# Slot sums of five tiles on VectorE in place of TensorE, 47 slots, and the weighting of three-slot units on ScalarE alone, in a graph attention kernel

One core of one Trainium2 chip. The metric is the device time of a whole execution, in microseconds, median of several runs; every run compared here is in the fast state (one run of e12 was over 1.5% above the fastest of its kernel and is left out of its ratio). A "point" is 1% of the time of before. "Before" and "after" are the kernels without and with the change.

## The reference

The reference is one layer of graph attention with a norm ahead of it, fp32 throughout, for 16 graphs (batches) of 1024 nodes with 512 features, 8 heads of 64. All batches share one adjacency matrix, which is sparse and has a few rows of high degree:

```python
_w = (1.0 + jnp.arange(1024)) ** -0.5; _w = _w / _w.mean()
_pij = jnp.clip(0.00390625 * _w[:, None] * _w[None, :], 0.0, 1.0)
adj = logical_or(uniform(1024, 1024) < _pij, eye(1024))
...
h = jnp.maximum(_layernorm(x), 0.0)
q, k, v = (h @ W + b for W, b in (Wq, Wk, Wv))            # as 8 heads of 64
scores = einsum('bihd,bjhd->bhij', q, k) / 8, where adj == 0: - 1e9
out = x + einsum('bhij,bjhd->bihd', softmax(scores), v)
```

## The kernel before

The kernel sorts the rows by degree, so that tile 0 (128 rows) holds the longest rows and tile 7 the shortest, and gives each tile as many neighbour slots as its longest row needs (`CAPS`). Lists of tile 0 that are longer still are cut into pieces of four, on 128 more rows (tile -1). One batch is 14 units of two to four slots. A unit passes these stations: GpSimd gathers one row of K and V per slot by an indirect DMA; VectorE multiplies K by the queries and sums over each head; ScalarE takes the exponent; VectorE (one slot) and ScalarE (the other slots) weight V; VectorE folds the slots into one; TensorE adds the units of a tile up in PSUM with an identity matrix; VectorE scales by the inverse row sum; GpSimd adds the input row and writes the output by an indirect DMA. Beside it TensorE projects the next batch.

```python
UNITS = ((7, 0, 2), (6, 0, 3), (5, 0, 4), (4, 0, 4), (3, 0, 3), (3, 3, 2), (2, 0, 3), (2, 3, 3),
         (1, 0, 4), (1, 4, 4), (0, 0, 4), (-1, 0, 4), (0, 4, 4), (0, 8, 4))     # tile, first slot, slots
BY_VECTOR = {2: 1, 3: 1, 4: 1}                # slots that VectorE weights
POOLS = dict(x=16, h=2, pht=1, hT=13, pkv=2, kvt=3, q=2, q0=1, g=5, acc=2, o=2)   # buffers

def fold(i, first, n):
    v = G[i][:, :, 1, :]
    nc.vector.tensor_tensor(v[:, 0:n], v[:, 0:n], v[:, first : first + n], ALU.add)
def add_up(i):                                # on TensorE
    ...
        nc.tensor.matmul(ACC[b, home], owner_t if t < 0 else ident, v[:, s, :], start=..., stop=...)
def row_sums(b, t):
    ...
    nc.vector.tensor_scalar(s, s, 2.0**-60, None, op0=ALU.max)
    nc.vector.reciprocal(INV[b, t], s)
def scale(b, t):
    nc.vector.tensor_mul(O[b, t]..., ACC.pop((b, t))..., INV.pop((b, t))...)   # per head
def residual(b, t):
    nc.gpsimd.tensor_tensor(O[b, t], O[b, t], X.pop(b * NT + NT - 1 - t), ALU.add)
def put_out(b, t):
    nc.gpsimd.indirect_dma_start(out=out_rows, out_offset=..., in_=O.pop((b, t))[:], ...)
```

The order in which every engine gets its instructions is not the order of the source. A planner (`Plan.ordered`) plays all steps through with guessed durations, priorities and buffer counts, and the kernel is emitted in the order that results. Each engine then works strictly in that order.

## Time and profile before

| | before |
|---|---|
| median of 3 runs | 1906.85 us (1903.21 to 1909.18) |
| TensorE, VectorE, ScalarE, GpSimd busy | 1764.5, 1749.3, 1420.9, 1292.4 us |
| mean granted TensorE clock | 0.983 |
| period of one batch in the middle | 110.2 us |

In lines of the profile PE is TensorE (PEld its weight loads), DVE is VectorE, ACT is ScalarE and POOL is GpSimd.

### The profile page before, as it was taken

The numbers are of one execution on the slowest core, as the hardware profiler recorded it, in microseconds if no ns is written. First come the engines' busy times: TensorE is split into PE (matmuls) and PEld (weight loads), VectorE is DVE, ScalarE is ACT, GpSimd is POOL, SyncE is SP. The second block draws the span as 40 slices with busy tenths as digits, with TensorE's granted clock in tenths as the row PEclk, the third lists the DMA queues.
The fourth block names the chain that finished last, engine by engine and source line by source line (L and its number), as shares of the span: only waits on it lengthen the run. The fifth ranks groups of instructions, "written<-read, shape, count | busy, mean of one in ns | idle before, by whom it ended". The sixth has DMA issues, their size and how long they took to land. (4 is left out here: it accounts for less than half of the span.)

```text
span 1906.6 us, 20253 instructions
## 1 busy us (share of the span) xinstructions
PE 1764.5 (93%) x4631; PEld 808.5 (42%) x4631; DVE 1749.3 (92%) x2330; ACT 1420.9 (75%) x5352; POOL 1292.4 (68%) x1244
## 2 busy tenths in 40 slices
PE   1799999999999999999999999999999999999884
PEld 0344444444444444444444444444444444444331
DVE  6759999999999999999999999999999999999995
ACT  2226777878788777877888787787778878777775
POOL 2616757677676867777676767778677767766673
PEclk9999999999999999999999999999999999999898
DMA  4628979888897988888898888889888888988873
GB/s 171 209 87 306 333 267 324 304 294 285 320 337 281 333 284 298 301 295 321 289 335 310 292 286 305 317 300 326 294 304 324 285 286 303 337 298 295 307 280 131
DMA packets 153951, 550.63 MB, mean 289 GB/s; under 512 B 18784, under 2 KB 18784, under 8 KB 153824
## 3 DMA queue, kind: packets, MB, share of 16 engines
q0 software_dynamic: 132224, 474.02, 71.0%
q1 hardware_dynamic: 21600, 75.24, 9.9%
q8 instruction: 39, 0.64, 0.1%
q14 instruction: 88, 0.72, 0.1%
HBM read 448.53 MB, written 100.66 MB: 288 GB/s over the span
## 5 line engine op out<-in xcount | busy, mean ns | idle before, releaser
L583 ACT ACTIVATE g<-g,weights 128x64 f32<-128x64 f32 x4352 | 1073.1, 338 | 0.0
L548 POOL DMA_INDIRECT g<-kv,index x768 | 763.2, 994 | 366.8 <-issue 247.7
L410 PE MATMUL pk<-wk,hT 128*128 128x512 f32 x1024 | 471.1, 604 | 0.0
L410 PE MATMUL pq<-wq,hT 128*128 128x512 f32 x1024 | 463.4, 596 | 0.0
L410 PE MATMUL pv<-wv,hT 128*128 128x512 f32 x1024 | 461.9, 594 | 0.0
L563 DVE TENSOR_REDUCE scores<-g 128x32 f32<-128x2048 f32 (+2 forms) x224 | 443.3, 1979 | 2.5
L558 DVE TENSOR_TENSOR g<-g,pq 128x2048 f32<-128x2048 f32 (+2 forms) x208 | 405.5, 1954 | 20.6 <-DMA g<-kv,index 14.6
L587 DVE TENSOR_TENSOR g<-g 128x512 f32<-128x512 f32 (+1 forms) x360 | 357.9, 994 | 7.9 <-ACT g L583 7.0
L602 PE MATMUL acc<-g,ident 128*128 128x512 f32 x538 | 274.8, 611 | 40.9 <-DVE g L587 33.0
L410 PEld LDWEIGHTS pk<-wk,hT 128*128 128x128 f32 x1024 | 200.0, 195 | 225.3 <-issue 221.2
L410 PEld LDWEIGHTS pv<-wv,hT 128*128 128x128 f32 x1024 | 195.8, 191 | 229.0 <-issue 225.6
L410 PEld LDWEIGHTS pq<-wq,hT 128*128 128x128 f32 x1024 | 196.5, 192 | 221.0 <-issue 217.4
L638 POOL DMA_INDIRECT out_dram<-o,perm x128 | 150.3, 1174 | 89.0 <-issue 68.8
L568 ACT ACTIVATE weights<-scores 128x32 f32<-128x32 f32 (+2 forms) x224 | 42.5, 190 | 223.9 <-DVE scores L564 223.5
L635 POOL TENSOR_TENSOR o<-o,x 128x512 f32<-128x512 f32 x128 | 165.1, 1291 | 23.0 <-DVE o L628 20.1
L366 POOL DMA_INDIRECT x<-in_x_dram,perm x128 | 143.8, 1124 | 53.0 <-issue 33.6
L602 PEld LDWEIGHTS acc<-g,ident 128*128 128x128 f32 x538 | 97.4, 194 | 146.2 <-issue 81.1
L577 DVE TENSOR_TENSOR g<-g,scores 128x512 f32<-128x512 f32 x224 | 152.3, 680 | 5.8 <-ACT scores L570 5.8
L393 ACT ACTIVATE h<-x,shift,rstd 128x512 f32<-128x512 f32 x128 | 103.5, 812 | 64.3 <-DVE shift L387 63.9
L421 ACT COPY kvt<-pk 128x512 f32<-128x512 f32 x128 | 73.4, 574 | 54.4 <-PE pk L410 48.3
L405 ACT COPY hT<-pht 128x512 f32<-128x512 f32 x128 | 74.4, 581 | 44.4 <-PE pht L400 44.4
L421 ACT COPY kvt<-pv 128x512 f32<-128x512 f32 x128 | 73.0, 570 | 45.7 <-PE pv L410 45.4
(149 smaller groups left out, 1036.8 us busy)
## 6 DMA issues: line engine op xcount, KB each, us to landing
kv<-kvt SPq DMA_DIRECT2D x128, 512.0 KB, 5.8
g<-kv,index POOLq DMA_INDIRECT x768, 6.3
adj<-in_adj_dram SPq DMA_DIRECT2D x8, 512.0 KB, 6.5
x<-in_x_dram,perm POOLq DMA_INDIRECT x128, 4.4
out_dram<-o,perm POOLq DMA_INDIRECT x128, 4.7
wk<-in_L_gnn_Wk_dram SPq DMA_DIRECT2D x1, 1024.0 KB, 11.2
wv<-in_L_gnn_Wv_dram SPq DMA_DIRECT2D x1, 1024.0 KB, 13.3
wq<-in_L_gnn_Wq_dram SPq DMA_DIRECT2D x1, 1024.0 KB, 12.7
```

What stands on the lines that cost most here:

```text
L366: nc.gpsimd.indirect_dma_start(out=X[n][:], out_offset=None, in_=x_rows, in_offset=on(ap=perm[:, t : t + 1], axis=0), element_offset=b * N * D
L410: nc.tensor.matmul(pt, HT[n][:, c, :], W[name][:, c, :], start=False, stop=(c == DC - 1))
L421: nc.scalar.copy(KVT[n][:, j, :], PT.pop((n, j)))
L548: nc.gpsimd.indirect_dma_start(out=G[i][:, s].rearrange("p j d -> p (j d)"), out_offset=None, in_=KV[b][:], in_offset=on(ap=index[:, c + s ...
L558: nc.vector.tensor_tensor(k, k, Q[b, t][:, None, :].to_broadcast([P, count, D]), ALU.mult)
L563: nc.vector.tensor_reduce(sc, heads(G[i][:, :count, 0, :]), AX.X, ALU.add)
L577: nc.vector.tensor_tensor(v, v, own.to_broadcast([P, n, H, HD]), ALU.mult)
L583: nc.scalar.activation(v[:, h, :], v[:, h, :], AF.Identity, scale=weights[:, c + s, h : h + 1])
L587: nc.vector.tensor_tensor(v[:, 0:n], v[:, 0:n], v[:, first : first + n], ALU.add)
L602: nc.tensor.matmul(ACC[b, home], owner_t if t < 0 else ident, v[:, s, :], start=(u == parts(home)[0] and s == 0), stop=(u == parts(home)[- ...
L635: nc.gpsimd.tensor_tensor(O[b, t], O[b, t], X.pop(b * NT + NT - 1 - t), ALU.add)
L638: nc.gpsimd.indirect_dma_start(out=out_rows, out_offset=on(ap=perm[:, t : t + 1], axis=0), in_=O.pop((b, t))[:], in_offset=None, element_o ...
```

## The change

The intent: TensorE and VectorE are level at the top; take the slot sums of tiles 7 to 3 off TensorE altogether (VectorE's fold leaves one slot per unit, so the scaling can read the gather buffer itself; the two units of tile 3 are joined by one more addition), and relieve VectorE by dropping the bound on row sums (one empty slot of weight 2^-60 per list does its work), one slot of 48, and the weighting of one slot in three-slot units, which goes to ScalarE. The planner is told, and replans; its guessed durations of folds and row sums change as well, which can move the order too (e4 below has these new guesses and is faster than before). The core of the diff:

```diff
-CAPS = (12, 8, 6, 5, 4, 4, 3, 2)
+CAPS = (11, 8, 6, 5, 4, 4, 3, 2)
-PIECES = 21
+PIECES = 17
-    (0, 8, 4),
+    (0, 8, 3),
+DIRECT = (7, 6, 5, 4, 3)
-BY_VECTOR = {2: 1, 3: 1, 4: 1}
+BY_VECTOR = {2: 1, 3: 0, 4: 1}
 ...  # in the plan
+        if by_vector(b, B, home):
+            acc = ("g", b * NU + parts[0])
+            added = weighed
+            if u != parts[0]:
+                added = [("join", i)]
+                add(("join", i), "DVE", 0.69, i + 1.5, weighed + summed, [g, acc])
+            summed = added
+        else:
+            add(("add_up", i), "PE", ...)
 ...
-    return {2: (), 3: ((2, 1), (1, 1)), 4: ((2, 2), (1, 1))}[count]
+    return {2: ((1, 1),), 3: ((2, 1), (1, 1)), 4: ((2, 2), (1, 1))}[count]
 ...
+def by_vector(b, B, t):
+    return t in DIRECT and b < B - 1
 ...
+        nc.gpsimd.memset(weights, 2.0**-60)
+        def join(i):
+            first = G[b * NU + parts_of(t)[0]][:, 0, 1, :]
+            nc.vector.tensor_tensor(first, first, G.pop(i)[:, 0, 1, :], ALU.add)
 ...
-            nc.vector.tensor_scalar(s, s, 2.0**-60, None, op0=ALU.max)
 ...  # in scale
+            if by_vector(b, B, t):
+                ACC[b, t] = G.pop(b * NU + parts_of(t)[0])[:, 0, 1, :]
```

More of the change, by code (lines that the diff above doesn't have):

```diff
@@ L39 @@
 SUM_MIN = 2.0**-30
-CAPS = (12, 8, 6, 5, 4, 4, 3, 2)
+CAPS = (11, 8, 6, 5, 4, 4, 3, 2)
 PIECE = 4
-PIECES = 21
+PIECES = 17
 LIST = CAPS[0] + PIECE * PIECES
+ROUNDS = -(-LIST // 8)
 UNITS = (
@@ L59 @@
     (0, 4, 4),
-    (0, 8, 4),
+    (0, 8, 3),
 )
+DIRECT = (7, 6, 5, 4, 3)
 UMAX = max(n for _, _, n in UNITS)
-SLOTS = sum(n for _, _, n in UNITS)
+SLOTS = sum(n for _, _, n in UNITS) + len(CAPS) + 1
 NU = len(UNITS)
 NT = len(CAPS)
-BY_VECTOR = {2: 1, 3: 1, 4: 1}
+BY_VECTOR = {2: 1, 3: 0, 4: 1}
 POOLS = dict(x=16, h=2, pht=1, hT=13, pkv=2, kvt=3, q=2, q0=1, g=5, acc=2, o=2)
@@ L171, in plan_of @@
         add(("list_of", t), "DVE", 2.6, -NU + 2 + 0.5 * t, [("sorted_rows", t)])
-    for k in range(LIST // 8):
+    for k in range(ROUNDS):
         add(("longest", k), "DVE", 2.4, -NU + 2.1 + 0.8 * k, [("longest", k - 1) if k else ("list_of", 0)])
-    add(("pieces",), "DVE", 9.0, -2, [("longest", LIST // 8 - 1)] + [("list_of", t) for t in range(NT)], [("pht", -1)], delay=1.0)
+    add(("pieces",), "DVE", 9.0, -2, [("longest", ROUNDS - 1)] + [("list_of", t) for t in range(NT)], [("pht", -1)], delay=1.0)
     for n in range(tiles):
@@ L217, in plan_of @@
         add(("exponent", i), "ACT", 0.4, i + 0.1, [("score", i)])
-        weighed = [("weigh_v", i)]
-        add(("weigh_v", i), "DVE", 0.15 + 0.533 * vector, i + 0.6, [("exponent", i)], [g])
+        weighed = []
+        if vector:
+            weighed.append(("weigh_v", i))
+            add(("weigh_v", i), "DVE", 0.15 + 0.533 * vector, i + 0.6, [("exponent", i)], [g])
         for s in range(count - vector):
@@ L223, in plan_of @@
         for n in folds(b, B, count):
-            add(("fold", i, *n), "DVE", 0.16 + 0.533 * n[1], i + 1.3, weighed, [g])
+            add(("fold", i, *n), "DVE", 0.2 + 0.6 * n[1], i + 1.3, weighed, [g])
             weighed = [("fold", i, *n)]
@@ L227, in plan_of @@
         acc = ("acc", b, home)
-        add(("add_up", i), "PE", 0.88 * (1 if folds(b, B, count) else count), i + 1.6, weighed, [g, acc])
-        parts = [v for v, (t_, _, _) in enumerate(UNITS) if max(t_, 0) == home]
+        parts = parts_of(home)
+        if by_vector(b, B, home):
[6 more added lines that the diff above has]
+        else:
+            add(("add_up", i), "PE", 0.88 * (1 if folds(b, B, count) else count), i + 1.6, weighed, [g, acc])
+            added = [("add_up", b * NU + v) for v in parts]
         if u == parts[-1]:
@@ L233, in plan_of @@
             sums = ("row_sums", b, home)
-            add(sums, "DVE", 0.6 if home else 1.2, i + 1, [("exponent", b * NU + v) for v in parts], [] if home else [("pht", -2, b)])
-            add(("scale", b, home), "DVE", 0.69, i + 1.8, [sums] + [("add_up", b * NU + v) for v in parts], [acc, o])
+            add(sums, "DVE", 0.4 if home else 1.0, i + 1, [("exponent", b * NU + v) for v in parts], [] if home else [("pht", -2, b)])
+            add(("scale", b, home), "DVE", 0.69, i + 1.8, [sums] + added, [acc, o])
             add(("residual", b, home), "POOL", 1.28, i + 2.5, [("scale", b, home)], [o, ("x", n)])
@@ L238, in plan_of, with parts_of @@
     return plan.ordered(POOLS)
+def parts_of(t):
+    return [u for u, (t_, _, _) in enumerate(UNITS) if max(t_, 0) == t]
+def by_vector(b, B, t):
+    return t in DIRECT and b < B - 1
 def folds(b, B, count):
@@ L437, in main_path @@
             col += count
+            if first + count == CAPS[tile_] or tile_ < 0:
+                col += 1
+        nc.gpsimd.memset(spot, 0.0)
         owner = const.tile([P, P], F32, tag="owner", name="owner")
@@ L448, in main_path @@
         ADJ = {}
-        found0 = const.tile([P, LIST + 1], F32, tag="found0", name="found_0")
+        found0 = const.tile([P, 8 * ROUNDS + 1], F32, tag="found0", name="found_0")
         def sorted_rows(t):
@@ L468, in longest @@
             nc.vector.max(found0[:, ts(k, 8)], row)
-            if k < LIST // 8 - 1:
+            if k < ROUNDS - 1:
                 nc.vector.match_replace(row, found0[:, ts(k, 8)], row, 0.0)
@@ L482, in pieces @@
             nc.tensor.matmul(before, below, count, start=True, stop=True)
-            begin = found[:, LIST : LIST + 1]
+            begin = found[:, 8 * ROUNDS : 8 * ROUNDS + 1]
             nc.vector.tensor_copy(begin, before)
@@ L491, in pieces @@
             nc.scalar.copy(owner_t, p_ot)
-            width = LIST + 1 - CAPS[0]
+            width = 8 * ROUNDS + 1 - CAPS[0]
             p_list = ps_h.tile([P, width], F32, tag="pht", name="p_list")
-            nc.tensor.matmul(p_list, owner, found[:, CAPS[0] : LIST + 1], start=True, stop=True)
+            nc.tensor.matmul(p_list, owner, found[:, CAPS[0] :], start=True, stop=True)
             part = once.tile([P, 1], F32, tag="part", name="part")
@@ L568, in exponent @@
             nc.scalar.activation(weights[:, w, :], scores[:, w, :], AF.Exp, scale=HD**-0.5)
-            own = scores[:, c + count - BY_VECTOR[count] : c + count, :]
-            nc.scalar.activation(own, own, AF.Exp, scale=HD**-0.5)
+            if BY_VECTOR[count]:
+                own = scores[:, c + count - BY_VECTOR[count] : c + count, :]
+                nc.scalar.activation(own, own, AF.Exp, scale=HD**-0.5)
         def weigh_v(i):
@@ L587, in fold @@
             nc.vector.tensor_tensor(v[:, 0:n], v[:, 0:n], v[:, first : first + n], ALU.add)
-        def parts(t):
-            return [u for u, (t_, _, _) in enumerate(UNITS) if max(t_, 0) == t]
+        def join(i):
+            b, t, w, c, count = unit(i)
+            first = G[b * NU + parts_of(t)[0]][:, 0, 1, :]
+            nc.vector.tensor_tensor(first, first, G.pop(i)[:, 0, 1, :], ALU.add)
         def add_up(i):
@@ L597, in add_up @@
             home = max(t, 0)
-            if u == parts(home)[0]:
+            if u == parts_of(home)[0]:
                 ACC[b, home] = ps_a.tile([P, D], F32, tag="acc", name=f"acc_{b}_{home}")
@@ L605, in add_up @@
                     v[:, s, :],
-                    start=(u == parts(home)[0] and s == 0),
-                    stop=(u == parts(home)[-1] and s == count - 1),
+                    start=(u == parts_of(home)[0] and s == 0),
+                    stop=(u == parts_of(home)[-1] and s == count - 1),
                 )
@@ L612, in row_sums @@
             c = first_col[t, 0]
-            nc.vector.tensor_reduce(s, weights[:, c : c + CAPS[t], :].rearrange("p s h -> p h s"), AX.X, ALU.add)
+            nc.vector.tensor_reduce(s, weights[:, c : c + CAPS[t] + 1, :].rearrange("p s h -> p h s"), AX.X, ALU.add)
             if t == 0:
@@ L645, in main_path @@
             sorted_rows, list_of, longest, pieces, load_x, stats, variance, power, shift, norm, flip, unflip, proj_kv, evict_kv,
-            store_kv, queries, copy_q, gather, multiply, score, exponent, weigh_v, weigh_s, fold, add_up, row_sums, scale,
+            store_kv, queries, copy_q, gather, multiply, score, exponent, weigh_v, weigh_s, fold, join, add_up, row_sums, scale,
             residual, put_out,
```

## The prediction

> **What bounds the kernel now.** First the page's table of busy time per engine.
>
> ```profile
> PE 1764.5 (93%) x4631; PEld 808.5 (42%) x4631; DVE 1749.3 (92%) x2330; ACT 1420.9 (75%) x5352; POOL 1292.4 (68%) x1244
> ```
>
> TensorE and VectorE are level, so a change that relieves only one of them should give little. The shares mix the start and the end with the middle, so I next asked for the busy time of each engine between 300 and 1700 us.
>
> ```profile
> core 0: us, PE busy (x) PEld busy (x) DVE busy (x) ACT busy (x) POOL busy (x), PEclk, DMA share, GB/s
> 300.00:1700.00 1400.00, 1359.79 (x3606) 625.52 (x3605) 1332.06 (x1750) 1115.27 (x4224) 1014.97 (x967) 0.99 0.86 306
> ```
>
> In the middle TensorE is busy 97.1%, VectorE 95.1%, ScalarE 79.7%, GpSimd 72.5% and the DMA engines 86%. To turn shares into time I need the period of one batch. One multiply per batch reads the queries of the split rows, so its starts, in the view of the gathered tile, mark the batches:
>
> ```profile
> L558 DVE TENSOR_TENSOR g<-g,pq_-1_1306 x1: 2275/2275/2275, 228.4 to 228.4; 128x2048 f32<-128x2048 f32 x1
> ...
> L558 DVE TENSOR_TENSOR g<-g,pq_-1_8974 x1: 2275/2275/2275, 1221.8 to 1221.8; 128x2048 f32<-128x2048 f32 x1
> ```
>
> Nine batches in 993.4 us: 110.4 us each. Of that TensorE is busy 107.2 and idle 3.2, VectorE busy 105.0 and idle 5.4, ScalarE busy 88.0. The waits of TensorE between 200 and 1780 us say what its small idle time is:
>
> ```profile
> PE acc L602 <- DVE g L587: 33.0, 11, 4.1
> PE p_more L619 <- DVE more L617: 6.0, 3, 2.1
> PE pq L408 <- DVE g L558: 3.8, 8, 0.6
> ```
>
> It waits for VectorE's folds, rarely. TensorE, in its fixed order, sets the pace, with VectorE 2 us per batch behind it.
>
> **What the skill says.** The Trainium skill, "TensorE: Matmul & The Clock Gate", section "Wait — 56ns, not 53.3ns?", gives a warm start-to-start of 215.7 ns for 512 columns. The trace shows an fp32 slot sum as two records, and this timeline shows what the pair occupies:
>
> ```profile
> 902.09 1.02 PE L602 MATMUL acc<-g,ident 128*128 128x512 f32 x2
> 902.95 0.60 PE L400 MATMUL pht<-ident,h 128*128 128x128 f32 x4
> ```
>
> The next matmul starts 0.86 us later, which is four times the skill's figure. I use 0.86, not the 2 x 611 ns of the group's mean durations, which overlap.
>
> "SBUF — State Buffer", section "Who interferes with whom", says that a VectorE instruction with two SBUF inputs contends with a GpSimd instruction that reads SBUF, and that `tensor_scalar` can enter a 2-port mode that contends too; the loser blocks. The trace agrees. The fold reads SBUF twice, the weighting reads SBUF and PSUM:
>
> ```profile
> L587 DVE TENSOR_TENSOR g<-g x360: 656/686/2873, 156.4 to 1801.0; 128x1024 f32<-128x1024 f32 x120, 128x512 f32<-128x512 f32 x60
> ...
> L577 DVE TENSOR_TENSOR g<-g,scores x224: 654/680/689, 147.3 to 1881.5; 128x512 f32<-128x512 f32 x112
> ```
>
> The weighting never takes over 0.689 us, the fold up to 2.873. The group means below hold these blocks, so I cost with means.
>
> "ScalarE: Activation LUTs", section "What ACT_TABLE_LOAD costs", says that an ACTIVATE costs a fixed part plus 0.833 ns per element and that back-to-back ones overlap by about 93 ns. In the trace one takes 338 ns, and a slot of eight takes 1.92 us (from 649.15 to the next instruction at 651.07), 240 ns each: 98 ns of overlap, in agreement.
>
> ```profile
> 649.15 2.01 ACT L583 ACTIVATE g<-g,weights 128x64 f32<-128x64 f32 x8
> 651.07 0.56 ACT L421 COPY kvt<-pk 128x512 f32<-128x512 f32 x1
> ```
>
> **The change part by part.** The durations, from the groups by shape:
>
> ```profile
> L587 DVE TENSOR_TENSOR g<-g 128x512 f32<-128x512 f32 x240 | 181.9, 758 | 1.3 <-ACT g L583 0.7
> L587 DVE TENSOR_TENSOR g<-g 128x1024 f32<-128x1024 f32 x120 | 176.0, 1467 | 6.6 <-ACT g L583 6.3
> ...
> L577 DVE TENSOR_TENSOR g<-g,scores 128x512 f32<-128x512 f32 x224 | 152.3, 680 | 5.8 <-ACT scores L570 5.8
> ...
> L628 DVE TENSOR_TENSOR o<-acc,inv 128x512 f32<-128x512 f32 x128 | 87.6, 684 | 6.2 <-PE acc L602 5.9
> ...
> L622 DVE TENSOR_SCALAR sums<-sums 128x8 f32<-128x8 f32 x128 | 50.4, 394 | 4.4
> ```
>
> The instruction orders of both kernels, compared by kind, give the counts.
>
> TensorE. In batches 0 to 14 the sums of tiles 7 to 3 went through it: 2 (two slots, unfolded) + 1 + 1 + 1 + 3 (one folded unit, one of two slots) = 8 fp32 matmuls per batch, 120 in all; one more goes in the last batch with the 48th slot. The orders agree: 269 become 148. 8 x 0.86 = 6.9 us per batch, 121 x 0.86 = 104 us in all. Nothing is added to TensorE.
>
> VectorE, per batch. Removed: eight bounds on row sums at 0.394 = 3.15. They are long because the 0.17 us instruction is blocked at times (median 0.172, longest 2.987). Five weightings of three-slot units (four units before, and the unit that shrinks from four slots to three) at 0.60, their spacing when they run back to back (0.68 less an overlap of 0.08) = 3.0. One slot of multiply and score: 2.284 less 1.749 and 2.281 less 1.756 = 1.06. A four-slot fold becomes a three-slot one: a wide and a narrow fold (1.467 + 0.758) become two narrow ones, 0.71. Added: folds of the two units of two slots, 2 x 0.758 = 1.52; the join of tile 3's two units, 0.758; five scalings that now read SBUF twice, by estimate as slow as a fold, 5 x (0.758 - 0.684) = 0.37. Net -7.92 + 2.65 = -5.3 us per batch. So VectorE takes over the sums and still loses work, since the bound and the weighting leave it at the same time. In the start two rounds of maximum and replacement go, 4 x 1.21 = 4.8 us.
>
> ScalarE. Four more slots per batch (34 become 38) x 1.92 = 7.7, less five small exponents that add 0.08 each to the spacing = 0.4: +7.3 us per batch, 117 in all. 88.0 becomes 95.3, still below the others.
>
> GpSimd and DMA. 16 fewer gathers of 768, at about 1.25 us per issue: 1.25 us per batch. The DMA share falls in bytes by 1.5% and rises per us as the period shrinks.
>
> Per batch TensorE then has 107.2 - 6.9 = 100.3, VectorE 105.0 - 5.3 = 99.7, ScalarE 95.3. If TensorE keeps its 3.2 of idle time, the period is 103.5; if VectorE keeps its 5.4, it is 105.1. I choose 104.6, nearer VectorE's, because it now owns more of the path and its waits for ScalarE get longer: a gain of 5.8 over 15 batches, 87 us. The shorter list at the start is worth some 2 of its 4.8, as TensorE is busy by then with projections of its own. The end costs some 4: the last batch still adds up on TensorE without folds, and from 1867 us on ScalarE runs there without a pause; its slots grow from 34 to 38, 7.7 us, of which I take half to be visible. 1906.9 - 87 - 2 + 4 = 1822; I say 1820.
>
> **The rivals.** (1) VectorE becomes the bound and gives the gain back: the scalings and joins read SBUF twice and are followed at once by GpSimd's residual (1.29 us), which reads SBUF as well. If each of the 8 new or changed instructions per batch is blocked for 0.3 us more, the period is 107.5 and the time about 1865. Against it: the folds, in the same neighbourhood, lose only 78 ns on average (758 against 680), and eight blocked bounds disappear. (2) ScalarE at 91% of the new period delays evictions and norms, so that TensorE waits for projection buffers: perhaps 2 us per batch, 1850. For it: 7.3 us more work in a fixed order, and units of three slots now wait for three slots in a row (5.8 us). Against it: TensorE has almost no waits for ScalarE now (1.5 us). (3) All waits fall: gathered buffers of direct tiles come free after VectorE's scaling rather than after TensorE's queue, on which the gathers waited 27.9 us in all, and TensorE's 33.0 us of waits for folds shrink with fewer sums. Then the full 104 us show, with the start: about 1798. (4) The gathers hide everything: at 86% DMA share already, 91% of a 104.6 us period. Against it: VectorE waits only 14.6 us in all for gathered data.
>
> **Range and chances.** TensorE's whole relief at the low end and rival 2 at the high end give 1795 to 1855. Faster by over 2% means below 1868.7, which even rival 1 would just pass; so 0.93. Within 2% needs two rivals at once, 0.06. Slower would need a fall into the slow general path or a broken pipeline; the row lists hold 79 neighbours and 128 pieces, and I counted at most 66 and 116 in the inputs, so 0.01.
>
> **What would show it.** Right: TensorE's busy time near 1660 us, VectorE's near 1660 (1749 less 15 x 5.3 and 4.8), ScalarE's near 1540; a period near 104.6 between the multiplies of the split rows; the scaling from SBUF near 0.76 us on average; the bounds gone. The step on VectorE is wrong if folds, joins and scalings average well above 0.76, the step on ScalarE if TensorE's waits for it exceed 20 us, the step on the end if the last batch takes over 10 us longer. The sum is wrong altogether if TensorE's idle time in the middle grows beyond 6 us per batch.

## More of the kernel before

From the view of VectorE's waits and from that of GpSimd's, kernel before, whole run (engine, tile and line; what ended the wait; us in total, times, longest):

```profile
DVE g L558 <- DMA g<-kv,index: 14.6, 4, 12.8
```

```profile
POOL out_dram L638 <- issue: 68.8, 49, 5.0
```

VectorE hardly ever waits for gathered rows. GpSimd stands 68.8 us ahead of output writes, and the profile sees nothing that it waits for ("issue"); the experiments show what it is in the kernel after.

## The result, and the profile after

| | before | after |
|---|---|---|
| median (runs of the same rounds, 4 each) | 1905.38 us | 1898.20 us |
| ratio, 95% interval | | 0.9956 (0.9934 to 0.9978) |
| mean granted clock | 0.983 | 0.969 |

The change is worth 0.4%, not 4.5%; the time lies outside the range. A ratio here and below is the mean time of one kernel's runs over that of before's runs of the same rounds, so it isn't quite the ratio of the medians; the ratios of the experiments also leave out the first, profiled run of each kernel.

The table of busy time of the kernel after, and its busy time between 300 and 1700 us (us, TensorE, weight loads, VectorE, ScalarE, GpSimd; clock; DMA share; GB/s):

```profile
PE 1682.0 (89%) x4343; PEld 766.7 (41%) x4389; DVE 1657.1 (88%) x2161; ACT 1529.8 (81%) x5784; POOL 1271.2 (67%) x1230
```

```profile
300.00:1700.00 1400.00, 1293.06 (x3353) 591.95 (x3390) 1264.95 (x1621) 1199.87 (x4565) 997.98 (x958) 0.97 0.83 302
```

The work left the engines as planned: VectorE fell by 92 us to 1657 (1660 was predicted), ScalarE rose to 1530 (1540), TensorE fell by 82 us to 1682 (1660; 46 of its 4389 matmul records are missing, so it is somewhat more). But they now stand idle instead: in the middle TensorE is busy 92.4% (97.1 before) and VectorE 90.4% (95.1). (37 of 3390 matmul records are missing in this window; at 0.43 us each, half of the 0.86 us pair, they would add about 1%, an estimate.) The batches' marks, the multiplies of the split rows, say so most directly:

```profile
L586 DVE TENSOR_TENSOR g<-g,pq_-1_1284 x1: 2281/2281/2281, 220.9 to 220.9; 128x2048 f32<-128x2048 f32 x1
...
L586 DVE TENSOR_TENSOR g<-g,pq_-1_8941 x1: 2273/2273/2273, 1212.6 to 1212.6; 128x2048 f32<-128x2048 f32 x1
```

Nine batches in 991.7 us: 110.2 us each, as before (110.4 over nine; over fourteen, 110.2 before and 110.0 after). **The period did not move.** The 14 us by which the span shrank are elsewhere: the first mark comes 7.5 us earlier, fourteen periods give 2.5, and the last batch and the end about 4.

What stands in the relief's place? First the waits of TensorE from 200 to 1780 us, then, over the whole run, the wait of VectorE for gathered rows and those of GpSimd ahead of output writes:

```profile
PE acc L634 <- DVE g L616: 43.3, 25, 6.2
PE acc L634 <- issue: 20.1, 7, 4.8
PE acc L634 <- ACT g L612: 12.1, 4, 4.5
PE pk L433 <- ACT hT L428: 9.9, 12, 1.7
PE pht L423 <- ACT h L416: 9.4, 7, 3.0
```

```profile
DVE g L586 <- DMA g<-kv,index: 99.9, 44, 13.9
```

```profile
POOL out_dram L670 <- issue: 98.6, 58, 5.5
...
POOL out_dram L670 <- DMA out_dram<-o,perm: 21.5, 7, 3.9
```

TensorE waits for everybody, VectorE waits seven times as long for gathered rows as before, and GpSimd waits longer ahead of output writes. Those go round in a ring: no row is gathered before a buffer is free, no buffer is free before VectorE has folded, and GpSimd issues the gathers behind its output writes. A view of waits can't say which link of such a ring is the guilty one. This piece of GpSimd's timeline (start, us, idle before it) shows one candidate:

```profile
597.84 2.51 POOL L667 TENSOR_TENSOR o<-o,x 128x512 f32<-128x512 f32 x2
600.51 1.29 POOL L670 DMA_INDIRECT out_dram<-o,perm  x1 [0.17 <-POOL o L667]
605.53 0.98 POOL L670 DMA_INDIRECT out_dram<-o,perm  x1 [3.73 <-issue]
```

Two output writes in a row: the second one stands still for 3.73 us after the first has been issued. In the built program every output write carries a wait for the DMA of the output write before it, since both write the same tensor. Counted from the order of GpSimd's instructions, the plan before has 2 such neighbours among its 127, the plan after 20; the idle time of GpSimd right ahead of output writes (gaps over 0.45 us, less 0.3 each) is 54 us before and 109 us after.

Last, the disputed costs on VectorE (count, total us, mean ns):

```profile
L616 DVE TENSOR_TENSOR g<-g 128x512 f32<-128x512 f32 x285 | 233.2, 818 | 5.2 <-ACT g L612 5.1
L616 DVE TENSOR_TENSOR g<-g 128x1024 f32<-128x1024 f32 x105 | 139.2, 1326 | 4.7 <-ACT g L612 4.5
...
L660 DVE TENSOR_TENSOR o<-g,inv 128x512 f32<-128x512 f32 x75 | 50.6, 674 | 5.3 <-DMA out_dram<-o,perm 5.0 <-issue 0.2
...
L622 DVE TENSOR_TENSOR g<-g,g 128x512 f32<-128x512 f32 x15 | 10.2, 683 | 0.0
```

The scaling from SBUF takes 674 ns, not the 758 of the prediction, and the join 683. The instructions that the change added are not slow.

### The profile page after: what moved, and what is told of

It is laid out like the page before. It is cut to its first block, busy times and chain, and to the rows that moved or that the text cites. A ratio compares the mean times of both kernels' runs of the same rounds, so it can differ in the third digit from the quotient of the medians.

```text
span 1892.6 us, 19830 instructions
## 1 busy us (share of the span) xinstructions
PE 1682.0 (89%) x4343; PEld 766.7 (41%) x4389; DVE 1657.1 (88%) x2161; ACT 1529.8 (81%) x5784; POOL 1271.2 (67%) x1230
## 5 line engine op out<-in xcount | busy, mean ns | idle before, releaser
L612 ACT ACTIVATE g<-g,weights 128x64 f32<-128x64 f32 x4864 | 1195.8, 338 | 1.5
L576 POOL DMA_INDIRECT g<-kv,index x752 | 751.9, 1000 | 341.3 <-issue 227.2
L586 DVE TENSOR_TENSOR g<-g,pq 128x2048 f32<-128x2048 f32 (+2 forms) x208 | 397.0, 1913 | 104.5 <-DMA g<-kv,index 99.9
L591 DVE TENSOR_REDUCE scores<-g 128x32 f32<-128x2048 f32 (+2 forms) x224 | 433.9, 1937 | 2.7 <-ACT scores L599 1.2
L616 DVE TENSOR_TENSOR g<-g 128x512 f32<-128x512 f32 (+1 forms) x390 | 372.4, 955 | 9.8 <-ACT g L612 9.6
L634 PE MATMUL acc<-g,ident 128*128 128x512 f32 x296 | 166.2, 658 | 95.3 <-DVE g L616 42.2
L634 PEld LDWEIGHTS acc<-g,ident 128*128 128x128 f32 x296 | 53.5, 201 | 172.6 <-issue 90.5
L423 PE MATMUL pht<-ident,h 128*128 128x128 f32 x512 | 82.9, 287 | 34.8 <-ACT h L416 34.0
L423 PEld LDWEIGHTS pht<-ident,h 128*128 128x128 f32 x512 | 66.5, 148 | 110.8 <-issue 53.7
L606 DVE TENSOR_TENSOR g<-g,scores 128x512 f32<-128x512 f32 x144 | 97.8, 680 | 4.0 <-ACT weights L596 2.4
```

The lines of the kernel that those rows point to most:

```text
L423: nc.tensor.transpose(PH[n][:, c, :], hn[:, ts(c, P)], ident)
L576: nc.gpsimd.indirect_dma_start(out=G[i][:, s].rearrange("p j d -> p (j d)"), out_offset=None, in_=KV[b][:], in_offset=on(ap=index[:, c + s ...
L586: nc.vector.tensor_tensor(k, k, Q[b, t][:, None, :].to_broadcast([P, count, D]), ALU.mult)
L591: nc.vector.tensor_reduce(sc, heads(G[i][:, :count, 0, :]), AX.X, ALU.add)
L612: nc.scalar.activation(v[:, h, :], v[:, h, :], AF.Identity, scale=weights[:, c + s, h : h + 1])
```

## The experiments

Theories: A, the output writes in pairs hold GpSimd. B, ScalarE is too full. C, VectorE's instructions with two SBUF inputs collide with GpSimd's. D, five gather buffers are too few. E, TensorE's idle time lowers its clock. F, the planner's order as a whole is at fault; G, the path of the data through VectorE is. H came later (see there).

The runs e1 to e10 and e13 to e16 were on one chip (13), e11 and e12 on a second (2), e17 and e18 on a third (10), none known to be that of the result. Each ratio is against runs of before on the same chip (medians 1922 to 1932 us).

**The kernel after, unchanged**, as the point that others are compared with.

> The changed kernel itself, unaltered, so that the experiments have it on their own chip. If chips agree: 0.996 of the kernel before. If theory A still holds and this chip is only worse for the changed kernel: 1.03 or more, as the run with side outputs was at 1.012 of before on the chip of the first four experiments.

1963.03 us, 1.0209 (1.0184 to 1.0233): on this chip the change makes the kernel 2% slower, where the first chip had it 0.4% faster. Before itself lost 0.9 to 1.0% between the two. The pattern is that of the first chip, with more idle time: TensorE busy 1272 of 1400 us (1293 there), clock 0.96 (0.97), 104 us of idle time ahead of output writes (109) and 177 ahead of gathers (119). So a gain or loss of two points of this kernel isn't a property of the code alone, and below only ratios of one chip are set against each other, but for the two kernels that were repeated.

**Output writes that don't wait for each other** (A). Tiles 1 to 7 write to DRAM tensors of their own; the order of instructions is kept, and the result is wrong.

```diff
-out=out_rows, ..., element_offset=b * N * D
+out=SIDE[t][:] if t else out_rows, ..., element_offset=0 if t else b * N * D
```

> The changed kernel, every instruction in the same order, but the outputs of tiles 1 to 7 go to seven separate buffers in device memory, so that a write of an output no longer waits for the write before it to land (wrong result on purpose). Theory A (GpSimd stands still for those landings, 110 us of gaps before output writes against 54 us before the change, and the gathers behind them come late): the gaps fall below 30 us, VectorE's wait for gathered data falls from 100 to below 40 us, the time to 1830 to 1860. Theory B (ScalarE, which got 7.3 us per batch more, delays TensorE): the gaps fall, the time stays above 1885. Theory C (VectorE's two-input reads collide with GpSimd): as B.

1943.38 us, 1.0124. The idle time ahead of output writes fell from 104 us to 2, so the waits are indeed those of one write for another, and VectorE's wait for gathered rows fell from 78 to 39.5 us. But 0.85 points, less than half of what A expected, is all that came of the 100 us: the idle time ahead of gathers rose from 177 to 265 us. What GpSimd waits for there isn't shown; free buffers are the likely reason.

**No two output writes in a row** (A, correct result). The planner makes each output write follow the one before it.

```diff
-[("residual", b, home)], [o], delay=4.0, moves=0.75)
+[("residual", b, home)] + ([put] if put else []), [o], delay=4.0, moves=0.75)
+put = ("put_out", b, home)
```

> The changed kernel with one more rule in the planner: an output write is placed only when the one before it has landed. Same instructions, other order, right result; no two output writes stand next to each other on GpSimd (20 pairs do in the changed kernel). Theory A: GpSimd's gaps before output writes fall from 110 us to below 50, time 1840 to 1870. Theories B and C: within 0.5% of the changed kernel, about 1895.

1945.97 us, 1.0108, no neighbours left, idle time ahead of output writes 23 us. It agrees with e1: theory A holds for about one point of the loss, and no more; the time that it had forecast wasn't reached.

**The weighting of three-slot units shared again** (B). `BY_VECTOR[3] = 1`, as in before.

> The changed kernel with one slot of each three-slot unit weighted on VectorE again (80 weightings back, 48 us; ScalarE loses 80 x 1.92 = 154 us). Theory A: no gain, 1895 to 1915, as the output writes are still in pairs (23). Theory B: faster, 1850 to 1875, because ScalarE is relieved. Theory C: 1895 to 1910.

1964.65 us, 1.0213 against 1.0209. ScalarE was relieved by 143 us (1534 to 1391 busy) and nothing came of it. By itself this doesn't settle B, since VectorE got 61 us more work (1718) and the plan changed too (23 neighbours among the output writes). The next run does: it leaves ScalarE at 1528 us and is far faster. Theory B falls, though TensorE's waits for ScalarE had grown.

**All sums on TensorE, the rest of the change kept.** `DIRECT = ()`; the planner replans.

> The changed kernel with the slot sums of all tiles on TensorE again (two-slot units still folded, no bound, 47 slots, three-slot units on ScalarE). TensorE gets 6 matmuls x 0.86 = 5.2 us per batch back, 77 us in all; output writes stand apart again (1 adjacent pair). Theory A: GpSimd's gaps before output writes back to about 55 us, time 1870 to 1890, not slower than the changed kernel although TensorE does more. Theory B: slower than the changed kernel or equal, 1895 to 1915, as ScalarE's load is the same. Theory C: faster than the changed kernel, 1860 to 1890, with the mean of a fold back from 818 to about 760 ns.

1883.98 us, 0.9792 (0.9771 to 0.9812): without its headline the change is worth 2.1%. Its window from 300 to 1700 us:

```profile
300.00:1700.00 1400.00, 1362.77 (x3630) 625.09 (x3629) 1267.20 (x1642) 1219.60 (x4658) 1005.73 (x969) 1.00 0.85 306
```

TensorE is busy 97.3% at full clock here. So five tiles' sums on VectorE cost 4.2 points on this chip, with all that they do to the plan.

**Six gather buffers** (D), two other pools made smaller for the room. The planner replans.

```diff
-hT=13, pkv=2, kvt=3, ... g=5
+hT=11, pkv=2, kvt=2, ... g=6
```

> The changed kernel with six buffers for gathered units in place of five (two fewer for transposed rows and one fewer for stored rows, which make the room). Theory D (the ring of gathered buffers sets the pace: on average 4.4 of 5 are held in the changed kernel, a unit holds one for 34 us): period falls toward 104 us per batch, time 1800 to 1850. Theory A alone: some gain, as this plan also has no two output writes next to each other, 1860 to 1880. If neither holds, about 1895.

1920.13 us, 0.9982, 2.3 points better than after. But the new plan also has no output writes in a row, so this run alone doesn't separate the buffer from the order.

**Direct sums for one-unit tiles only.** `DIRECT = (7, 6, 5, 4)`: no join.

> The changed kernel with direct sums for tiles 7, 6, 5 and 4 alone; tile 3, whose first buffer waits through the join for its second unit, goes back to TensorE (2 matmuls per batch, 26 us). Theory D: the long hold of that buffer (41.7 us against a mean of 34.2) is gone, time 1870 to 1890. Theory A: 15 adjacent pairs of output writes are left of 20, time within 0.5% of the changed kernel.

1949.97 us, 1.0154, 0.55 points better than after. The plan has 15 neighbours among its output writes in place of 20; the join is not the main cost.

**TensorE kept busy** (E). The kernel after in its own order, plus one constant fp32 matmul on TensorE, read by nobody, for each of the 90 sums that left it (batches 0 to 14, one per unit).

```diff
+nc.tensor.matmul(WARM[b, home], ident, W["q"][:, 0, :], start=..., stop=...)
```

> The changed kernel, all engines in the same order, plus 6 fp32 matmuls per batch (90 in all, 77 us) of constant data on TensorE where the slot sums used to stand; nobody reads their result. Theory E (TensorE's time is no longer on the path, and its idle gaps lower its granted clock, 0.97 against 0.99): time within 0.5% of the changed kernel or up to 1% faster, clock back at 0.98 or more. If TensorE were still the bound: slower by up to 77 us, 1960 to 1975.

1979.82 us, 1.030, 0.9 points slower than after. 90 x 0.86 = 77 us of work were added to TensorE and the time rose by 17, so TensorE's work isn't what the others follow here, for the most part. (The idle sums also take turns with the real ones in two buffers of PSUM, which may be a part of the 17.) E's own expectation was missed too: the time is more than 0.5% longer, and the clock rose from 0.961 to 0.969 only, not to 0.98.

**Order against path of the data** (F, G). Two runs cross them. e9: direct sums, but every instruction in the order that the planner makes for sums on TensorE; a join stands where the second unit's sum stood. e10: the order of the kernel after, but with sums on TensorE.

```diff
 # e9
+for key in plan.ordered(POOLS):           # planned as if all sums were on TensorE
+    if key[0] == "add_up" and by_vector(b, B, home):
+        if u == parts_of(home)[0]: continue
+        key = ("join", key[1])
+    order.append(key)
```

> The work of the changed kernel (direct sums for tiles 7 to 3) in the order that the planner made for the kernel with all sums on TensorE (0.979 of before); on each engine every other instruction stands where it stands there, and a join stands where the add-up stood. Theory F (the direct sums themselves cost nothing; the planner's order for them is worse, among other things because it knows nothing of output writes waiting for each other): 0.96 to 0.98 of before. Theory G (the data path is worse: VectorE holds the gathered buffers, reads SBUF twice, and must do itself what TensorE did beside it): 1.00 to 1.03 of before, as the changed kernel on this chip (1.021).

> The other corner: the order that the planner made for the changed kernel, but the sums of tiles 7 to 3 done on TensorE right after the last fold, and scaled from PSUM. Theory F: as slow as the changed kernel or slower, 1.02 to 1.04 of before (TensorE has 5.2 us per batch more). Theory G: near 0.98 of before, as with the other order.

| ratio on chip 13 | sums on VectorE | sums on TensorE |
|---|---|---|
| in the order of after | 1.0209 (e5) | 1.0552 (e10) |
| in the order of the plan for TensorE | 0.9863 (e9) | 0.9792 (e4) |

The windows of e9 and e10:

```profile
300.00:1700.00 1400.00, 1317.62 (x3448) 598.77 (x3447) 1242.10 (x1650) 1214.71 (x4636) 1019.68 (x964) 0.98 0.86 304
```

```profile
300.00:1700.00 1400.00, 1281.97 (x3290) 578.94 (x3290) 1183.05 (x1498) 1119.47 (x4237) 920.02 (x885) 0.96 0.78 279
```

**The order is worth 3.5 points with the same direct sums, and 7.6 with the same sums on TensorE.** That is theory F in the main, though e9 lies a little above its range (0.98) and e10 above its own. One reserve belongs to the 7.6: the order of after has no place for the sums on TensorE, and e10 puts each right behind its fold, so TensorE's waits for folds there (60.8 us between 200 and 1780 us, 6.5 in e4) can be the placement's. The 3.5 has no such flaw. In the better order the direct sums still give nothing against e4 (+0.7 points), though TensorE has 77 us less to do. TensorE stands at 91.6% in e10 with exactly the work that makes it 97.3% busy in e4.

**The better order with six buffers**, sums on TensorE (e11) and direct (e12).

> The rest of the change with the sums on TensorE (0.979 on this chip with five gather buffers), now with six gather buffers of 16 KB (one from the transposed rows, 13 to 11, and one from the projections' rows, 3 to 2). If the ring of gathered buffers (D) is what still holds this version: 0.965 to 0.972, with TensorE over 97% busy in the middle. If this version is at TensorE's limit already (it was 97.3% busy in the middle at a clock near 1.00): 0.975 to 0.985, no gain, and more gather buffers held without effect. If the planner's order for six buffers happens to be a bad one: above 0.99.

> The direct sums in the order that the planner makes for the sums on TensorE, with six gather buffers (the order of the run beside it). If direct sums have been held by the ring and by the order together, this is the version where TensorE's 77 us fewer should show at last: 0.955 to 0.97, and it beats the run beside it. If TensorE's work no longer sets the pace and the loop from gather to fold does even with six buffers: 0.98 to 0.99, as the direct sums with five buffers in the same kind of order (0.986), and equal to or slower than the run beside it.

1863.13 us, 0.9662 (0.9618 to 0.9706), and 1923.24 us, 0.9941 (0.9864 to 1.0017). The windows of e11 and of e12:

```profile
300.00:1700.00 1400.00, 1379.02 (x3652) 636.98 (x3704) 1301.68 (x1670) 1248.51 (x4765) 1040.21 (x993) 1.00 0.88 313
```

```profile
300.00:1700.00 1400.00, 1305.82 (x3374) 598.26 (x3411) 1287.10 (x1631) 1202.75 (x4583) 998.17 (x957) 0.97 0.86 303
```

e11 lies where D expected it, is correct and beats before by 3.4%, with TensorE 98.5% busy. Against e4 it gains 1.3 points, from chip to chip and in a new plan, so the buffer and the order aren't separated here any more than in e6. e12 lies outside both expectations: with six buffers the direct sums lose 2.8 points at one and the same order. That miss led to the next theory. The two runs were repeated on a third chip:

> The sums on TensorE with six buffers again, unchanged. On another chip it was 0.966. If the gain of the one-input residual there (0.954) was the edit's: 0.963 to 0.969 on the same chip, so the edit is worth about 1.2 points. If it was the chip's: 0.952 to 0.957.

> The direct sums in the other order with six buffers again, unchanged. On another chip it was 0.994. If the gain of the one-input residual (0.963) was the edit's: 0.985 to 0.998 on the same chip. If it was the chip's: 0.960 to 0.970.

1861.90 us, 0.9644, and 1919.75 us, 0.9964, both in the range for "the edit's" (the edit is that of e14 and e15 below). These two kernels keep their ratios within 0.3 points from chip to chip.

**What differs between e11 and e12 on VectorE** are the same instructions at different lengths. From the groups by shape, the folds of e11, and then e12:

```profile
L616 DVE TENSOR_TENSOR g<-g 128x512 f32<-128x512 f32 x285 | 204.2, 717 | 11.1 <-ACT g L612 4.9 <-issue 2.2 <-ACT weights L596 2.1
L616 DVE TENSOR_TENSOR g<-g 128x1024 f32<-128x1024 f32 x105 | 128.4, 1223 | 6.5 <-ACT g L612 6.0 <-issue 0.5
```

```profile
L626 DVE TENSOR_TENSOR g<-g 128x512 f32<-128x512 f32 x285 | 218.9, 768 | 11.6 <-remote 5.9 <-ACT g L622 4.9 <-issue 0.2
L626 DVE TENSOR_TENSOR g<-g 128x1024 f32<-128x1024 f32 x105 | 152.7, 1454 | 4.2 <-ACT weights L606 1.8 <-ACT g L622 1.7 <-issue 0.6
L670 DVE TENSOR_TENSOR o<-g,inv 128x512 f32<-128x512 f32 x75 | 61.7, 823 | 0.0
L413 DVE TENSOR_SCALAR rstd<-mv 128x2 f32<-128x2 f32 x64 | 32.9, 515 | 0.1
```

The scaling from SBUF, 674 ns in after, takes 823 in e12. Setting folds against GpSimd's instructions by their times in the trace: those that overlap a residual addition (two SBUF inputs, 1.3 us) are stretched, the others aren't (wide folds of e12 with over 0.1 us of overlap: 1.87 us on average, the rest 1.21). 75 of 390 overlap in e12 and 28 in e11, at one and the same order, so it is the timing that decides. That is theory H, a part of C. It can be tested with every instruction in its place: give GpSimd's instruction one SBUF input. The result is wrong.

```diff
-nc.gpsimd.tensor_tensor(O[b, t], O[b, t], X.pop(...), ALU.add)
+nc.gpsimd.tensor_scalar(O[b, t], X.pop(...), 1.0, None, op0=ALU.mult)
```

> The kernel after, with GpSimd's residual addition turned into a copy of the x rows by a multiplication with 1 (one input from SBUF in place of two; wrong result on purpose, every instruction stands where it stood). The kernel after was 1.021 on this chip. H (folds that coincide with the two-input addition are stretched): 52 folds lose about 0.97 us each, 50 us in all, in a loop that VectorE belongs to, so about 30 to 50 us fall away: 0.995 to 1.005, and the folds' mean falls from 0.95 to about 0.82 us. If the coincidence is real but hidden in waits: 1.015 to 1.025 with the shorter folds. If GpSimd's copy stretches folds as much: folds' mean unchanged, and no change of time.

> The direct sums in the other order with six buffers (0.994), with the same edit. H: 75 folds lose 0.84 us each there, 63 us, or 3.3 per cent: 0.965 to 0.975, the same as or a little faster than the sums on TensorE in that order with the same edit. If the data path of the direct sums (VectorE's in-order joins and scalings, gather buffers held longer) is what costs: 0.985 to 0.995 in spite of the shorter folds.

> Control: the sums on TensorE in that order with six buffers (0.966), with the same edit. Only 28 folds coincide there, 0.27 us each or 8 us, and TensorE is 98.5% busy: H expects 0.960 to 0.966. If the edit speeds a kernel in some way that has nothing to do with folds (GpSimd's own time), this run falls as much as the other two, to 0.945.

> The direct sums in the other order with six buffers (0.994), with one constant matmul on TensorE for each sum that left it, so TensorE has the work of e11 again, unread. If TensorE's idle gaps and lower clock (0.97 against 1.00) cost the time: 0.97 to 0.985. If TensorE is no longer what sets the pace and folds or the data path are: 0.99 to 1.005. If TensorE's own time still bounds (its work adds up): 1.01 to 1.03.

| | without the edit | with it | gain, points | VectorE busy, us |
|---|---|---|---|---|
| after | 1.0209 (e5) | 1.0034 (e13) | 1.8 | 1657 to 1611 |
| direct, better order, six buffers | 0.9941, 0.9964 (e12, e18) | 0.9627 (e14) | 3.2 | 1675 to 1610 |
| on TensorE, better order, six buffers | 0.9662, 0.9644 (e11, e17) | 0.9541 (e15) | 1.1 | 1639 to 1596 |

The last two rows compare chips (without the edit 2 and 10, with it 13). Chip 13 has one run near the second row's left side: e16, the kernel of e12 with idle matmuls on top, at 0.9985.

The same groups in e14:

```profile
L626 DVE TENSOR_TENSOR g<-g 128x512 f32<-128x512 f32 x285 | 201.8, 708 | 27.2 <-ACT g L622 11.6 <-issue 10.6 <-remote 4.3
L626 DVE TENSOR_TENSOR g<-g 128x1024 f32<-128x1024 f32 x105 | 131.7, 1254 | 4.5 <-ACT g L622 3.2 <-issue 0.8
L670 DVE TENSOR_TENSOR o<-g,inv 128x512 f32<-128x512 f32 x75 | 52.5, 699 | 0.0
L413 DVE TENSOR_SCALAR rstd<-mv 128x2 f32<-128x2 f32 x64 | 15.7, 245 | 0.1
```

In e14 VectorE's 65 us (folds 38, the norm's `rstd` 17, scaling 9) show almost whole in the time (3.2% of 1925 is 62 us). Its time is a little below the range of H, but it stays behind e15, which H didn't expect. e13 gave back 34 of 46 us, in the range expected; the folds' mean fell from 950 to 850 ns (820 was expected). The control, e15, fell by more than was expected of its folds alone (10 us): there the two-column instructions of the norm, which I hadn't counted, got 34 us shorter as well. Half of VectorE's 43 us shows; TensorE is 99.5% busy in the middle. So H is shown, with two limits. Before was never run with the edit, so these runs don't say that the change lost time by collisions (see the rivals below). And the edit also changes GpSimd's own instruction (1.29 to 1.64 us in e14, longer), and what that does by itself wasn't measured.

e16, at 0.9985 against 0.994 and 0.996 of e12 and e18 (on other chips), says that 77 us of TensorE work come and go in the direct version for 0.2 to 0.4 points, with the clock up from 0.96 to 0.98. The expectation for "TensorE is no longer what sets the pace" is met; that a higher clock would save time (E) isn't seen.

VectorE's busy time in e9, in the better order, is 1614 us, as low as the edit makes that of after (1611), which suggests that most of e13's 1.8 points belong to what the orders differ by.

What stays open: about 0.9 of the 3.5 points between the orders if the gains of e1 (0.85) and e13 (1.8) add up, which wasn't tried in one kernel; why the direct sums remain 0.7 to 0.9 points behind at equal order even where collisions are few (e9 against e4) or cut down (e14 against e15); what holds the direct sums in e9, where the gain is 1.4% and not 4.5; and why after is at 0.996 on one chip and 1.021 on another.

## Why the prediction was wrong

**The step that failed** is the one from busy time to period: "If TensorE keeps its 3.2 of idle time, the period is 103.5; if VectorE keeps its 5.4, it is 105.1". Neither kept it. Per batch TensorE's idle time grew from 3.2 to 8.4 us and VectorE's from 5.4 to 10.6 (7.6% and 9.6% of 110.0): nearly the whole relief turned into waiting (of TensorE's 8.4, about 1.3 are missing records, by the estimate above). The prediction had named the sign, "idle time in the middle grows beyond 6 us per batch", and it came. What the runs put in the step's place:

- The order is a part of the change. The prediction compared the orders of the two kernels for counts of instructions and not for what stands next to what. Order alone moves this kernel by 3.5 points with direct sums (e5, e9). On that chip the change fell about 6.6 points short of the forecast (1.021 for 0.954), so the order is about half of the shortfall, and the other half, which e9 still shows, stays open. Of the 3.5, output writes that wait for each other are about 0.9 (e1, e2: 1.0), and GpSimd's two-input additions up to 1.8 (e13).
- Most of TensorE's 104 us were not on the path once they had gone. Adding 77 us (4 points) back in two direct versions cost 0.9 and 0.2 to 0.4 points (e7, e16). "TensorE, in its fixed order, sets the pace" fits kernels with TensorE above 97%, as before, e4 and e11 are, and not one where it is relieved. What sets the pace there isn't shown: the loop from gather to fold was the guess, but a sixth buffer in it didn't help the direct sums (0.986 in e9, 0.994 and 0.996 in e12 and e18).
- The clock took a part as well: 0.99 to 0.97 in the middle, about 2% of TensorE's 1293 us. That is 26 us, about the difference between the 104 us expected and the 82 seen (the missing records make the true fall smaller still). In e7 and e16 more work on TensorE raised the clock, and no time was saved, so the clock followed the idle time more than it caused it.

Step by step: the counts and the busy times of VectorE (1657 for 1660) and ScalarE (1530 for 1540) were right. On VectorE some luck was in it: narrow folds took 818 ns for 758 (17 us more in 285), wide ones 1326 for 1467 (15 less in 105), scalings 674 for 758 (6 less in 75). The period, -87 us, was -2.5. The start, -2 us, was -7.5 (first mark). The end, +4, was about -4: the last batch took 2.2 us less and the rest 1.8 less.

The rivals: (1), VectorE blocked, fails as told, since scalings and joins took 674 and 683 ns in after. Its mechanism is real in the folds, in the norm's two-column instructions and, in another order, in the scaling (823 ns), and taking it away is worth 1.1 to 3.2 points (e13 to e15). But it is no cost that the change brought. Added up from the traces (durations of VectorE's instructions less the undisturbed length of their group), the stretching is 83 us before, 66 after, 63 in e5 and 19 in e9: before had more of it, 28 us in the bounds that were dropped, and would by this gain from the one-input addition too, which wasn't run. "Only 78 ns on average" hides that a few folds are hit hard (19 of 240 narrow ones before, by about 1 us each), and a replanned order draws that lot again, for better (e9) or worse. (2), ScalarE: TensorE's waits for it passed the 20 us of the prediction (12.1 + 9.9 + 9.4 = 31), but relieving it by 143 us gave nothing (e3), and with ScalarE just as full e4 is 4.2 points faster: a symptom. (3), all waits fall, is what didn't happen. (4), the gathers: VectorE's wait for them grew from 14.6 to 99.9 us, but the DMA share fell from 0.86 to 0.83, and e11 moves 313 GB/s where after moves 302. From issue to landing a gather took 6.6 us in the median (6.3 before). So rows came late mainly because they were asked for late.

## What to carry to other kernels

When two engines are level and a planner sets a fixed order, price the new order too: count which instructions became neighbours on the in-order queue that feeds the loop (here output writes on GpSimd), and which pairs on two engines now overlap. To learn what a change does by itself, run it in the old order and the old work in the new order; here that showed in two runs that the order cost 3.5 points and the headline part gained nothing, and that the rest of the change with one more buffer was worth 3.4 to 3.6%. Work taken off a full engine is a gain only until the next loop is reached: add idle work back, and if the time hardly moves, the engine had left the path.

## What the Trainium skill lacked or had wrong

- "SBUF — State Buffer", section "Who interferes with whom", has it that a VectorE instruction with two SBUF inputs contends with a GpSimd instruction that reads SBUF. The runs agree for two-input additions on GpSimd, but one that reads one SBUF input stretched the folds far less: wide folds 1454 to 1254 ns, narrow ones 768 to 708 (e12, e14). The page makes no difference between one and two inputs of GpSimd (the edit changed the operation too, from an addition to a multiplication).
- The same section counts `tensor_scalar` among those that can block. It has no number for tiny ones: one over 128x2 elements took 515 ns in e12 and 245 in e14, 17 us in 64 instructions.
- "TensorE: Matmul & The Clock Gate", section "What's actually happening", lets TensorE's clock fall to half after at least one idle window of about 3.4 us. The clock records in the traces agree on the half and the window: the 0.97 of after is full clock with 13 stretches of half clock between 300 and 1700 us, of 3.4 to 17.1 us. But no wholly idle window was needed: e9 has 15 such stretches there, and TensorE's longest idle time is 3.2 us. The section doesn't say how little is enough.
- No page that I read says that two indirect writes to one DRAM tensor stand in a row on GpSimd if the program makes the second wait for the first: here 3.7 us of idle time for the pair shown; ahead of all output writes 104 us in e5, and 2 us with separate tensors (e1).
- No page says how far one kernel's gain may differ between chips: 0.996 and 1.021 for the kernel after, while two others agreed within 0.3 points on two chips.
